# Linear attention's causal part: sub-chunks of 64 tokens in 32x64 and 64x32 TensorE tiles, two chunks at a time

## The chip, the core and the metric

The kernel runs on one core of a Trainium2 chip. The metric is the device time of one execution in microseconds (us). A core has five engines that run side by side, each through its own instruction queue in order: TensorE (PE: matrix products into PSUM, with its weight loads, PEld), VectorE (DVE), ScalarE (ACT), GpSimd (POOL) and SyncE (SP, which issues the DMAs here). PSUM, where TensorE writes, has 8 banks of 512 f32 columns on 128 partitions.

## What is computed

Four blocks, one after another, on 8 sequences of 1024 tokens with 256 features; each block adds to its input. The first is a decoder layer with linear attention (16 heads of 16) and a dense part of width 1024, the second a dense part of width 1024, the third softmax attention with one head of 256, the fourth a gated dense part of width 704 whose operands are rounded to a 4-bit format. The change is in the attention of the first block:

```python
q = sigmoid(heads(Wq, bq)); k = sigmoid(heads(Wk, bk)); v = heads(Wv, bv)
...                                            # scales from running sums of q and k
qs = q * (sink_in / normal)[..., None]
vs = v * src_comp[..., None]
kv = jnp.cumsum(jnp.einsum('bhld,bhlm->bhldm', k, vs), axis=2)
x  = jnp.einsum('bhld,bhldm->bhlm', qs, kv) * sink_alloc[..., None]
```

For token l this is the sum over all earlier tokens and itself of (qs_l . k_j) vs_j, head by head. A kernel splits it by chunks of tokens: inside a chunk the scores k.q are computed and cut to the causal triangle, and everything before the chunk enters through one carried state, the sum of k times vs (16 x 16 per head).

## The kernel before

All work is written as Python generators ("parts"), which ask for an engine, operands, PSUM banks and buffers; `Plan.run` picks, one after another, the part that can go on soonest by its own table of costs (`Plan.took`), so the order of the instructions on all engines is fixed when the program is built. Every instruction is issued through one helper, so that nearly all have one line in the profile (342); tile names tell them apart. Three things in the planner matter below. A need may carry `banks=n` and waits until so many banks are free. `took` counts a matmul with at most 32 rows or columns of weights as a quarter of a full one, and adds 0.2 where tiled and full matmuls follow each other; `run` lets tiled work follow tiled work. Where it expects TensorE to wait for more than 1.6 us, `fill` puts matmuls of the identity (bank<-ident in the profile) into the gap, one for each 0.22 of pause - 0.7.

Tokens go in chunks of 128 (`P`); four chunks make a group (`G`), so a sequence has two groups and the whole 16 (`flows`, p). `linear_group` and `linear_span` compute q, k and the scales of one group, with the running sums on DVE in buffers of kind "flow" (512 columns wide, nine of them). Then `linear_chunk` does the causal part for each of the four chunks, and beside it the dense parts (`dense`: w_in, w_out, hidden), the softmax attention and the last block (`soft_chunk`: wqk, qT, prob, vt, wgT, wuT, wdT) of earlier groups go on.

`linear_chunk` (line 1147) in order:
- v of the chunk (bank<-wv,n0T), plus bias, times its scale, into one of four `v_pads`, whose heads stand in 32 columns of which 16 are zero;
- qz, two copies of q with either the even or the odd heads set to zero (ACT, two of 256 columns);
- scores: for each of four row tiles (32 rows, two heads) and both halves k of the features a matmul of 32 rows by 128 columns with 256 columns moving, into four banks (bank<-qz,k, 8 matmuls);
- DVE multiplies each bank by the triangle `triu` into a flow buffer (sc<-bank,triu, four of 512 columns). In the first group ACT does it, with a large negative triangle (`later`, bf16) put into the bank first and a Relu;
- k is turned (two transposes and an ACT copy), except in a sequence's last chunk;
- into one bank: the carried state times q (bank<-q,kv_sum, 8 matmuls of 128 rows by 32 columns, 128 moving), then the chunk's own part (bank<-sc,v_pad, 16 of the same shape), and into its other columns the chunk's update of the state (bank<-v_pad,k, 8, 32 columns moving);
- ACT copies the result out (xo), DVE multiplies the update by the block diagonal (kv<-bank,bdiag), and POOL adds it to the carried sum in a new tile (kv_sum);
- the output projection (bank<-wo,xo), layer norm and the turn of the result for the dense part.

`count["attended"]` keeps the chunks in their order.

## Time and profile before

| | |
|---|---|
| median of 3 runs | 2615.89 us (2615.59 to 2617.68) |
| the profiled execution | 2618.8 us |
| its span, first to last instruction | 2617.1 us |
| granted TensorE clock, mean | 0.997 |
| evictions sc<-bank,triu on DVE | 240 of 680 ns |
| kv<-bank,bdiag on DVE | 56 of 420 ns |
| kv_sum adds on POOL | 48 of 728 ns (median) and 8 copies of 396 ns |
| bank<-ident on TensorE | 274 records, 35.1 us busy |

The profile is of one execution on the chip. It lists busy time by engine and by group of instructions: "out<-in" are the program's tile names, then the shape of the tile of weights (rows*columns), the output shape, the number of records, busy us and mean ns of one. Matmuls are pipelined, so a record's ns is its length from start to end, while the next one starts long before; busy us counts overlapping records once. PEld is the load of weights that goes with each matmul. Times in the timeline are us from the span's start.

### The profile page before, as it was taken

What the parts mean: (1) busy time and instruction counts of PE and PEld (TensorE: products, weight loads), DVE (VectorE), ACT (ScalarE), POOL (GpSimd) and SP (SyncE); (2) the same over time, 40 slices, a digit from 0 to 9 for tenths busy, and PEclk for the clock granted to TensorE, in tenths of its full rate; (3) what the DMA queues carried; (4) which work ended last, traced back from release to release, by engine and by line L of the source; (5) the groups of instructions that cost most, each with busy time, mean ns of one, the idle gap of its engine ahead of it and who ended that gap; (6) DMA issues with size and microseconds to landing.
All of it is one profiled execution on the core that took longest, in us unless ns stands there. A gap on an engine that the chain in (4) does not pass through costs nothing.

```text
span 2617.1 us, 46326 instructions
## 1 busy us (share of the span) xinstructions
PE 2571.5 (98%) x16593; PEld 2010.4 (77%) x16593; DVE 1947.3 (74%) x4352; ACT 1344.0 (51%) x2658; POOL 703.0 (27%) x1293
## 2 busy tenths in 40 slices
PE   8998999999999999999999999999999999999999
PEld 7777777877777777777877877777777777878777
DVE  6788796867769587685868768677785877855687
ACT  3535636464475544645555464645545545454443
POOL 2343332332313232131321322313231231311000
PEclk9999999999999999999999999999999999999999
DMA  2445443333323342322433323333333423333100
GB/s 75 125 121 154 115 117 95 109 88 107 86 80 101 85 115 68 108 80 85 117 81 92 97 75 99 92 108 81 99 82 83 115 72 96 88 87 89 31 5 21
DMA packets 391268, 237.11 MB, mean 91 GB/s; under 512 B 129152, under 2 KB 379520, under 8 KB 391040
## 3 DMA queue, kind: packets, MB, share of 16 engines
q1 hardware_dynamic: 391040, 234.16, 33.1%
q8 instruction: 132, 2.16, 0.4%
q14 instruction: 96, 0.79, 0.1%
HBM read 188.17 MB, written 20.71 MB: 80 GB/s over the span
## 4 chain that ended last, share of the span: by engine, by line
PE 80%; DVE 13%; ACT 3%; DMA 1%; issue 1%; POOL 1%; SPq 0%; DVEq 0%; POOLq 0%; ACTq 0%
PE bank L342 80%; DVE hid L342 2%; DVE prod L342 2%; DVE n L342 1%; ACT L342 1%; DVE ln_st L342 1%; DVE u L342 1%; DVE res L342 1%; DVE ln_mv L342 0%; DVE x_amax L342 0%; DMA spread<-packed 0%; DVE div L342 0%; DVE spread L342 0%; DVE mx L342 0%; DMA spun<-cut 0%
## 5 line engine op out<-in xcount | busy, mean ns | idle before, releaser
L342 PE MATMUL bank<-half,w_in 128*128 128x256 f32 x2048 | 533.4, 384 | 7.3 <-DVE v L342 4.5
L342 PE MATMUL bank<-w_out,hidden 128*128 128x256 f32 x2048 | 529.4, 383 | 2.7 <-DMA w_out<-in_L_ffn_w_dram 1.6
L342 POOL TENSOR_SCALAR ln_ve<-ln_mv 128x1 f32<-128x1 f32 x384 | 96.9, 252 | 1607.8 <-DVE ln_mv L342 1591.3
L342 PEld LDWEIGHTS bank<-w_out,hidden 128*128 128x128 f32 x2048 | 374.0, 190 | 105.2 <-issue 53.2
L342 PEld LDWEIGHTS bank<-half,w_in 128*128 128x128 f32 x2048 | 384.3, 191 | 85.6 <-issue 22.5
L342 ACT ACT_TABLE_LOAD x321 | 411.8, 1283 | 17.3 <-DVE nmax L342 11.6
L342 ACT ACTIVATE hidden<-bank,c_L_ffn_b 128x256 f32<-128x256 f32 x256 | 120.6, 472 | 269.4 <-PE bank L342 269.1
L342 POOL TENSOR_TENSOR ln_rstd<-ln_ve,neghalf 128x1 f32<-128x1 f32 x384 | 236.3, 615 | 32.0
L342 PE MATMUL bank<-n2T,qT 128*128 128x512 f32 x512 | 241.6, 594 | 0.4 <-ACT qT L342 0.2
L342 PE MATMUL bank<-vt,probT 128*128 128x256 f32 x1024 | 232.0, 380 | 0.0
L342 PEld LDWEIGHTS bank<-vt,probT 128*128 128x128 f32 x1024 | 193.1, 190 | 30.2 <-issue 3.0
L342 ACT ACTIVATE hidden<-bank,c_L_attn_b 128x256 f32<-128x256 f32 x256 | 119.7, 468 | 183.3 <-PE bank L342 182.8
L342 PE MATMUL bank<-wdT,hqT 128*128 128x256 f32 x768 | 176.6, 380 | 1.2 <-ACT hqT L342 1.0
L342 PE MATMUL bank<-wgT,xqT 128*128 128x352 f32 x512 | 173.8, 462 | 0.0
L342 PE MATMUL bank<-wuT,xqT 128*128 128x352 f32 x512 | 172.4, 459 | 0.0
L342 ACT COPY half<-spun 128x512 uint16<-128x512 uint16 x128 | 86.3, 674 | 150.1 <-DMA spun<-cut 149.6
L342 PEld LDWEIGHTS bank<-wdT,hqT 128*128 128x128 f32 x768 | 145.3, 190 | 22.7 <-ACT hqT L342 1.4
L342 DVE TENSOR_TENSOR sc<-bank,triu 128x512 f32<-128x512 f32 x240 | 149.7, 680 | 8.5 <-PE bank L342 8.0
L342 PEld LDWEIGHTS bank<-n2T,qT 128*128 128x128 f32 x512 | 93.4, 190 | 69.1 <-issue 60.5
L342 PEld LDWEIGHTS bank<-wuT,xqT 128*128 128x128 f32 x512 | 97.4, 190 | 54.1
L342 DVE TENSOR_TENSOR hid<-hid,bank 128x352 f32<-128x352 f32 x116 | 59.7, 515 | 101.4 <-PE bank L342 79.2
L342 PEld LDWEIGHTS bank<-wgT,xqT 128*128 128x128 f32 x512 | 93.7, 190 | 37.1 <-issue 4.3
(220 smaller groups left out, 4530.2 us busy)
## 6 DMA issues: line engine op xcount, KB each, us to landing
w_in<-in_L_attn_W_dram SPq DMA_DIRECT2D x256, 128.0 KB
w_out<-in_L_attn_W_dram SPq DMA_DIRECT2D x256, 128.0 KB
w_in<-in_L_ffn_w_dram SPq DMA_DIRECT2D x256, 128.0 KB
w_out<-in_L_ffn_w_dram SPq DMA_DIRECT2D x256, 128.0 KB
spread<-packed SPq DMA_DIRECT2D x90, 256.0 KB
x<-in_L_attn_inputs_dram SPq DMA_DIRECT2D x64, 128.0 KB
xr<-in_L_attn_inputs_dram SPq DMA_DIRECT2D x64, 128.0 KB
rows<-res SPq DMA_DIRECT2D x64, 128.0 KB
```

The lines of the kernel that those rows point to most:

```text
L342: ins = method(*args, **kw)
```

## The change

A chunk of 128 is cut into two sub-chunks of 64 (u = 0, 1), and two chunks (n = 0, 1) are done in one part, `linear_pair`. Scores are computed only inside a sub-chunk: 32 rows by 64 columns of weights, 128 columns moving (both heads' copies of 64 tokens), sub-chunk u on partitions 64u to 64u+63, the four row tiles in four banks; one bank now holds both chunks, so DVE masks four banks for a pair, with a triangle of 64 by 64. The update of the state is computed for each of the four sub-chunks, in tiles of 64 rows by 32 columns, before the scores; DVE brings it out in two operations (one per u, both chunks), and POOL turns the four updates into four running states, in place, one add after another. The chunk's own part takes 64 rows by 32 columns with 64 columns moving, and then each sub-chunk adds its state times q, 128 rows by 32 columns, 64 moving. The two u write two banks, and two ACT copies put them together in xo. What follows, `linear_rest`, is as before for each chunk. The turning of k moves ahead of the scores, and happens for all chunks.

Buffers: six of kind flow instead of nine, three of a new kind kvs, five weight buffers (`W_FF`) instead of four for each of w_in and w_out. The planner's table counts a tile's share of the array, with a least cost of 0.0136, and 0.2 at each change of tile shape.

```diff
-W_FF = 4
+W_FF = 5
...
-    "flow": (9, 512, F32),
+    "flow": (6, 512, F32),
+    "kvs": (3, 512, F32),
...
-            tiled = op == "matmul" and (kw["lhsT"].shape[-1] <= 32 or kw["lhsT"].shape[0] <= 32)
-            if tiled or op == "matmul" and kw["lhsT"].dtype == BF16:
-                cost *= 0.25
+                if rows * cols < P * P and kw["lhsT"].shape[-1] > 1:
+                    tiled = rows, cols
+                    cost = max(cost * rows * cols / (P * P), 0.0136)
...
+        yield pe(*pads, *kTs, *[t for t, _ in qzs], banks=2, tiled=True)
+        kvbanks = [mm_bank()[:, :D].rearrange("p (c k d) -> p c k d", c=2, k=2) for _ in range(2)]
+        for n in range(2):
+            for k in range(2):
+                for r in range(4):
+                    for u in range(2):
+                        sub = slice(64 * u, 64 * u + 64)
+                        nc.tensor.matmul(
+                            kvbanks[u][32 * r : 32 * r + 32, n, k, :32],
+                            lhsT=kTs[n][sub, k, 32 * r : 32 * r + 32],
+                            rhs=v_columns(pads[n][sub], range(4 * k + r, 4 * k + r + 1)),
...
+        yield pe(banks=4, tiled=True)
         banks = [mm_bank() for _ in range(4)]
...
-        for r, bank in enumerate(banks):
-            rows = slice(32 * r, 32 * r + 32)
+        for n in range(2):
             for k in range(2):
-                nc.tensor.matmul(
-                    bank[:, k * D : (k + 1) * D],
-                    lhsT=qk[1][rows, k, here],
-                    rhs=qz[rows, k, :, :],
+                for u in range(2):
+                    for r, bank in enumerate(banks):
+                        rows = slice(32 * r, 32 * r + 32)
+                        t0 = pair[n] * P + 64 * u
+                        nc.tensor.matmul(
+                            bank[64 * u : 64 * u + 64, n * D + k * P : n * D + (k + 1) * P],
+                            lhsT=qk[1][rows, k, t0 : t0 + 64],
+                            rhs=qzs[n][1][rows, k, :, 64 * u : 64 * u + 64],
...
+        for m in range(3 if end else 4):
+            before, after_ = states[m][1], states[m + 1][1]
+            if before is not None:
+                yield plan.pool(*[t for t, _ in states[m : m + 2]])
+                nc.gpsimd.tensor_tensor(after_, before, after_, ALU.add)
...
+        outs = [mm_bank()[:, :D].rearrange("p (c k t) -> p c k t", c=2, k=2) for _ in range(2)]
+        for n in range(2):
             for k in range(2):
+                for e in range(2):
+                    for r in range(4):
+                        for u in range(2):
+                            sub = slice(64 * u, 64 * u + 64)
+                            nc.tensor.matmul(
+                                outs[u][32 * r : 32 * r + 32, n, k, :],
+                                lhsT=pads[n][sub, 8 * k + 2 * r + e, :],
+                                rhs=scores[r][sub, n, k, e, :],
...
+        for n in range(2):
+            for u in range(2):
+                state = states[2 * n + u][1]
+                if state is None:
+                    continue
+                t0 = pair[n] * P + 64 * u
+                for k in range(2):
+                    for r in range(4):
+                        nc.tensor.matmul(
+                            outs[u][32 * r : 32 * r + 32, n, k, :],
+                            lhsT=state[:, k, 32 * r : 32 * r + 32],
+                            rhs=qk[0][:, k, t0 : t0 + 64],
```

More of the change, by code (lines that the diff above doesn't have):

```diff
@@ L181, in took @@
             cost = size * (0.853e-3 if op == "transpose" else 1.687e-3)
-            tiled = op == "matmul" and (kw["lhsT"].shape[-1] <= 32 or kw["lhsT"].shape[0] <= 32)
-            if tiled or op == "matmul" and kw["lhsT"].dtype == BF16:
-                cost *= 0.25
+            tiled = False
+            if op == "matmul":
+                rows, cols = (kw["lhsT"].shape[0], kw["lhsT"].shape[-1])
+                rows, cols = (min([n for n in (32, 64, P) if n >= x] + [P]) for x in (rows, cols))
+                if rows * cols < P * P and kw["lhsT"].shape[-1] > 1:
+                    tiled = rows, cols
+                    cost = max(cost * rows * cols / (P * P), 0.0136)
+                elif kw["lhsT"].dtype == BF16:
+                    cost *= 0.25
             if tiled != self.tiled:
@@ L465, in block_stack_kernel @@
     make_block_diagonal(tc.nc, bdiag, DH)
-    triu = const.tile([P, P], F32, name="triu")
-    make_upper_triangular(tc.nc, triu)
+    triu = const.tile([P, 64], F32, name="triu")
+    for u in range(2):
+        make_upper_triangular(tc.nc, triu[64 * u : 64 * u + 64])
     v_pads = [const.tile([P, H, 32], F32, name=f"v_pad{i}") for i in range(V_PADS)]
@@ L534, in late_constants @@
         nc.vector.tensor_scalar(
-            later[:, :GT].rearrange("p (n t) -> p n t", n=4),
-            triu.unsqueeze(1).to_broadcast([P, 4, P]),
+            later[:, :GT].rearrange("p (n t) -> p n t", n=8),
+            triu.unsqueeze(1).to_broadcast([P, 8, 64]),
             -1.0,
@@ L1143, in linear_span, with linear_pair @@
         plan.start(scaled(), p + 0.55 + after)
-        for i in span:
-            plan.start(linear_chunk(p, i, n0T, comp, qk), p + 0.55 + 0.03 * i + after)
-    def linear_chunk(p, i, n0T, comp, qk):
+        for j in range(span.start // 2, span.stop // 2):
+            plan.start(linear_pair(p, j, n0T, comp, qk), p + 0.55 + 0.06 * j + after)
+    def linear_pair(p, j, n0T, comp, qk):
         s, g = divmod(p, NG)
-        past, c = seqs[s]["past"], p * G + i
-        at = p - (p == 0 and i < 2)
-        here = slice(i * P, (i + 1) * P)
-        yield pe(
-            n0T,
-            banks=1,
-            when=lambda: count["v"] == c and c - count["attended"] < V_PADS and "v" in late,
-        )
-        bank = mm_bank()
-        for k in range(2):
-            nc.tensor.matmul(
-                bank[:, :D],
-                lhsT=n0T[:, k, here],
-                rhs=wqkv[2][:, k, :],
-                start=k == 0,
-                stop=k == 1,
-            )
-        count["v"] += 1
-        pad = v_pads[c % V_PADS]
-        v = yield from fresh("lin", dve(bank), "v")
-        nc.vector.tensor_tensor(v, bank[:, :D], bv1, ALU.add)
-        yield dve(comp)
-        nc.vector.tensor_tensor(
-            v_columns(pad, range(H // 2)),
-            v.rearrange("p (j e d) -> p j e d", e=2, d=DH),
-            comp[:, i, H:].rearrange("p (j e) -> p j e", e=2).unsqueeze(3)
-            .to_broadcast([P, H // 2, 2, DH]),
-            ALU.mult,
-        )
-        plan.drop(v)
-        tile_qz = yield from fresh(
-            "flow",
-            act(
-                qk[0],
-                at=at + 0.62 + 0.06 * i,
-                when=lambda: i in groups[p]["scaled"]
-                and count["scored"] == c
-                and c - count["attended"] < 2,
-            ),
-            "qz",
-        )
-        count["scored"] += 1
-        qz = tile_qz.rearrange("p (k e t) -> p k e t", k=2, e=2)
-        by_act = p == 0
-        for e in range(2):
-            nc.scalar.activation(
-                qz[:, :, e, :], qk[0][:, :, here], AF.Copy, scale=parity[:, e : e + 1]
-            )
-        yield pe(qz, *([later] if by_act else []), banks=4, tiled=not by_act)
@@ new lines, in linear_pair @@
+        past, c = seqs[s]["past"], p * G + 2 * j
+        at = p - (p == 0 and j == 0)
+        pair = (2 * j, 2 * j + 1)
+        pads, kTs = [], []
+        end = g == NG - 1 and j == G // 2 - 1
+        for n, i in enumerate(pair):
+            here = slice(i * P, (i + 1) * P)
+            yield pe(
+                n0T,
+                banks=1,
+                at=at + 0.55 + 0.06 * i,
+                when=lambda: count["v"] == c + n
+                and c + n - count["attended"] < V_PADS
+                and "v" in late,
+            )
+            bank = mm_bank()
+            for k in range(2):
+                nc.tensor.matmul(
+                    bank[:, :D],
+                    lhsT=n0T[:, k, here],
+                    rhs=wqkv[2][:, k, :],
+                    start=k == 0,
+                    stop=k == 1,
+                )
+            count["v"] += 1
+            pad = v_pads[(c + n) % V_PADS]
+            pads.append(pad)
+            v = yield from fresh("lin", dve(bank), "v")
+            nc.vector.tensor_tensor(v, bank[:, :D], bv1, ALU.add)
+            yield dve(comp)
+            nc.vector.tensor_tensor(
+                v_columns(pad, range(H // 2)),
+                v.rearrange("p (j e d) -> p j e d", e=2, d=DH),
+                comp[:, i, H:].rearrange("p (j e) -> p j e", e=2).unsqueeze(3)
+                .to_broadcast([P, H // 2, 2, DH]),
+                ALU.mult,
+            )
+            plan.drop(v)
@@ new lines, in linear_pair @@
+        for n, i in enumerate(pair):
+            yield pe(
+                banks=1,
+                at=at + 0.62 + 0.06 * i,
+                when=lambda: i in groups[p]["scaled"] and count["attended"] == c,
+            )
+            bank = turned([qk[1][:, k, i * P : (i + 1) * P] for k in range(2)])
+            kT = two((yield from fresh("lin", act(bank), "k")))
+            nc.scalar.copy(kT, bank)
+            kTs.append(kT)
+        qzs = []
+        by_act = p == 0
+        for n, i in enumerate(pair):
+            tile_qz = yield from fresh("flow", act(qk[0], at=at + 0.64 + 0.06 * i), "qz")
+            qz = tile_qz.rearrange("p (k e t) -> p k e t", k=2, e=2)
+            for e in range(2):
+                nc.scalar.activation(
+                    qz[:, :, e, :],
+                    qk[0][:, :, i * P : (i + 1) * P],
+                    AF.Copy,
+                    scale=parity[:, e : e + 1],
+                )
+            qzs.append((tile_qz, qz))
@@ new lines, in linear_pair @@
+        kv = past.get("kv")
+        sums = [None, None]
+        yield pe(*pads, *kTs, *[t for t, _ in qzs], banks=2, tiled=True)
[9 more added lines that the diff above has]
+                            rhs=v_columns(pads[n][sub], range(4 * k + r, 4 * k + r + 1)),
+                            start=n == 0 and k == 0,
+                            stop=True,
+                            skip_group_check=True,
+                        )
@@ L1201, in linear_chunk @@
+        plan.drop(*kTs)
+        yield pe(banks=4, tiled=True)
         banks = [mm_bank() for _ in range(4)]
@@ L1207, in linear_chunk @@
                 )
-        for r, bank in enumerate(banks):
-            rows = slice(32 * r, 32 * r + 32)
+        for n in range(2):
             for k in range(2):
-                nc.tensor.matmul(
-                    bank[:, k * D : (k + 1) * D],
-                    lhsT=qk[1][rows, k, here],
-                    rhs=qz[rows, k, :, :],
-                    start=not by_act,
-                    stop=True,
-                    skip_group_check=True,
-                )
-        plan.drop(tile_qz)
+                for u in range(2):
[6 more added lines that the diff above has]
+                            rhs=qzs[n][1][rows, k, :, 64 * u : 64 * u + 64],
+                            start=not by_act,
+                            stop=True,
+                            skip_group_check=True,
+                        )
+        plan.drop(*[t for t, _ in qzs])
+        for u in range(2):
+            new = yield from fresh("kvs", dve(kvbanks[u]), "kv")
+            new = sums[u] = new.rearrange("p (c k d) -> p c k d", c=2, k=2)
+            nc.vector.tensor_tensor(
+                new.rearrange("p c k (r d) -> p (c k) r d", r=4),
+                kvbanks[u][:, :, :, :32].rearrange("p c k d -> p (c k) d")
+                .unsqueeze(2).to_broadcast([P, 4, 4, 32]),
+                bdiag.rearrange("p (r d) -> p r d", r=4).unsqueeze(1).to_broadcast([P, 4, 4, 32]),
+                ALU.mult,
+            )
+        states = [(kv, kv if kv is None else kv[:, 1])]
+        for m in range(4):
+            tile_ = sums[m % 2]
+            states.append((tile_, tile_[:, m // 2]))
+        for m in range(3 if end else 4):
[3 more added lines that the diff above has]
+                nc.gpsimd.tensor_tensor(after_, before, after_, ALU.add)
+        past["kv"] = sums[1]
         scores = []
@@ L1222, in linear_chunk @@
             sc = yield from fresh("flow", (act if by_act else dve)(bank), "sc")
-            sc = sc.rearrange("p (n t) -> p n t", n=4)
+            scores.append(sc.rearrange("p (c k e t) -> p c k e t", c=2, k=2, e=2))
+            sc = sc.rearrange("p (n t) -> p n t", n=8)
             if by_act:
-                nc.scalar.activation(sc, bank.rearrange("p (n t) -> p n t", n=4), AF.Relu)
-                scores.append(sc)
+                nc.scalar.activation(sc, bank.rearrange("p (n t) -> p n t", n=8), AF.Relu)
                 continue
@@ L1229, in linear_chunk @@
                 sc,
-                bank.rearrange("p (n t) -> p n t", n=4),
-                triu.unsqueeze(1).to_broadcast([P, 4, P]),
+                bank.rearrange("p (n t) -> p n t", n=8),
+                triu.unsqueeze(1).to_broadcast([P, 8, 64]),
                 ALU.mult,
             )
-            scores.append(sc)
-        end = g == NG - 1 and i == G - 1
-        if not end:
-            yield pe(banks=1, at=at + 0.66 + 0.06 * i, when=lambda: count["attended"] == c)
-            bank = turned([qk[1][:, k, here] for k in range(2)])
-            kT = two((yield from fresh("lin", act(bank), "k")))
-            nc.scalar.copy(kT, bank)
-        kv = past.get("kv")
         yield pe(
-            pad,
+            *pads,
             *scores,
-            *([] if kv is None else [kv]),
-            *([] if end else [kT]),
-            banks=1,
+            *[t for t, _ in states[:4] if t is not None],
+            banks=2,
             tiled=True,
@@ L1250, in linear_chunk @@
         )
-        kv = past.get("kv")
-        both = mm_bank()
-        plan.keep(both)
-        bank = both[:, :D]
-        for k in range(2):
-            for r in range(4):
-                if kv is not None:
-                    nc.tensor.matmul(
-                        bank[32 * r : 32 * r + 32, k * P : (k + 1) * P],
-                        lhsT=kv[:, k, 32 * r : 32 * r + 32],
-                        rhs=qk[0][:, k, here],
-                        start=k == 0,
-                        stop=False,
-                        skip_group_check=True,
-                    )
@@ L1268, in linear_chunk @@
-        for k in range(2):
-            for e in range(2):
-                for r in range(4):
-                    nc.tensor.matmul(
-                        bank[32 * r : 32 * r + 32, k * P : (k + 1) * P],
-                        lhsT=pad[:, 8 * k + 2 * r + e, :],
-                        rhs=scores[r][:, 2 * k + e, :],
-                        start=kv is None and k == 0 and e == 0,
-                        stop=k == 1 and e == 1,
-                        skip_group_check=True,
-                    )
@@ L1279, in linear_chunk @@
-        plan.drop(*scores)
-        if not end:
-            kvbank = both[:, D : D + 64].rearrange("p (k d) -> p k d", k=2)
-            for k in range(2):
-                for r in range(4):
-                    nc.tensor.matmul(
-                        kvbank[32 * r : 32 * r + 32, k, :],
-                        lhsT=kT[:, k, 32 * r : 32 * r + 32],
-                        rhs=v_columns(pad, range(4 * k + r, 4 * k + r + 1)),
-                        start=False,
-                        stop=True,
-                        skip_group_check=True,
-                    )
-            plan.drop(kT)
@@ L1294, in linear_chunk @@
-        xo = two((yield from fresh("lin", act(bank), "xo")))
-        nc.scalar.copy(xo, two(bank))
-        if not end:
-            new = two((yield from fresh("lin", dve(kvbank), "kv")))
-            nc.vector.tensor_tensor(
-                new.rearrange("p k (r d) -> p k r d", r=4),
-                kvbank.unsqueeze(2).to_broadcast([P, 2, 4, 32]),
-                bdiag.rearrange("p (r d) -> p r d", r=4).unsqueeze(1).to_broadcast([P, 2, 4, 32]),
-                ALU.mult,
-            )
-            plan.let_go(both)
-            yield plan.pool(new)
-            total = past["kv"] = wk.tile([P, 2, P], F32, tag="kv_sum", name="kv_sum", bufs=2)
-            if kv is None:
-                nc.gpsimd.tensor_copy(total, new)
-            else:
-                nc.gpsimd.tensor_tensor(total, kv, new, ALU.add)
-            plan.drop(new)
-        else:
-            plan.let_go(both)
@@ L1314, in linear_chunk @@
-        count["attended"] += 1
-        if by_act and i == G - 1:
-            plan.drop(later)
-        yield pe(xo, banks=1, at=at + 0.7 + 0.06 * i, when=lambda: "chunk" in late)
+        outs = [mm_bank()[:, :D].rearrange("p (c k t) -> p c k t", c=2, k=2) for _ in range(2)]
+        for n in range(2):
+            for k in range(2):
+                for e in range(2):
+                    for r in range(4):
+                        for u in range(2):
+                            sub = slice(64 * u, 64 * u + 64)
[3 more added lines that the diff above has]
+                                rhs=scores[r][sub, n, k, e, :],
+                                start=n == 0 and k == 0 and e == 0,
+                                stop=False,
+                                skip_group_check=True,
+                            )
@@ new lines, in linear_pair @@
+        for n in range(2):
+            for u in range(2):
+                state = states[2 * n + u][1]
+                if state is None:
+                    continue
+                t0 = pair[n] * P + 64 * u
+                for k in range(2):
+                    for r in range(4):
+                        nc.tensor.matmul(
+                            outs[u][32 * r : 32 * r + 32, n, k, :],
+                            lhsT=state[:, k, 32 * r : 32 * r + 32],
+                            rhs=qk[0][:, k, t0 : t0 + 64],
+                            start=False,
+                            stop=True,
+                            skip_group_check=True,
+                        )
@@ new lines, in linear_pair @@
+        plan.drop(*scores, sums[0])
+        if kv is not None:
+            plan.drop(kv)
+        if end:
+            plan.drop(sums[1])
+        xo = yield from fresh("flow", act(*outs), "xo")
+        xo = xo.rearrange("p (c k t) -> p c k t", c=2, k=2)
+        for u in range(2):
+            nc.scalar.copy(xo[:, :, :, 64 * u : 64 * u + 64], outs[u])
+        count["attended"] += 2
+        if by_act and j == G // 2 - 1:
+            plan.drop(later)
+        left = [2]
+        for n, i in enumerate(pair):
+            plan.start(linear_rest(p, i, xo, xo[:, n], left), at + 0.7 + 0.06 * i)
@@ L1318, in linear_chunk, with linear_rest @@
+    def linear_rest(p, i, tile_xo, xo, left):
+        at = p - (p == 0 and i < 2)
+        yield pe(tile_xo, banks=1, when=lambda: "chunk" in late)
         bank = mm_bank()
@@ L1322, in linear_chunk @@
             )
-        plan.drop(xo)
+        left[0] -= 1
+        if not left[0]:
+            plan.drop(tile_xo)
         count["linear"] += 1
```

## The prediction

> **What bounds the kernel now.** I read the page's shares of busy time first, then the groups of TensorE instructions by form, then the timeline of one chunk, then narrow windows inside its bursts.

> ```profile
> span 2617.1 us, 46326 instructions
> PE 2571.5 (98%) x16593; PEld 2010.4 (77%) x16593; DVE 1947.3 (74%) x4352; ACT 1344.0 (51%) x2658; POOL 703.0 (27%) x1293
> PE 80%; DVE 13%; ACT 3%; DMA 1%; issue 1%; POOL 1%; SPq 0%; DVEq 0%; POOLq 0%; ACTq 0%
> ```

> TensorE is busy for 98% of the span and carries 80% of the chain that ended last; the other engines have room (74%, 51%, 27%). So time that TensorE no longer needs comes off the end nearly one for one, as long as the instruction order keeps feeding it. The groups that the change touches:

> ```profile
> L342 PE MATMUL bank<-qz,k 32*128 32x256 f32 x1024 | 75.6, 400 | 1.3 <-ACT qz L342 1.3
> L342 PE MATMUL bank<-sc,v_pad 128*32 128x128 f32 x2048 | 67.8, 273 | 0.0
> L342 PE MATMUL bank<-q,kv_sum 128*32 128x128 f32 x896 | 36.1, 279 | 0.0
> L342 PE MATMUL bank<-v_pad,k 128*32 128x32 f32 x896 | 17.3, 195 | 0.0
> ```

> Together 197 us busy, 7.5% of the span. An f32 matmul of the program is two records (64 chunks x 8 score matmuls are x1024). The timeline shows what one chunk costs, start to start:

> ```profile
> 1004.88 1.06 PE L342 MATMUL bank<-n2T,wqk 128*128 128x128 f32 x8
> 1005.86 0.65 PE L342 MATMUL bank<-q,kv_sum 128*32 128x128 f32 x16
> 1006.33 1.06 PE L342 MATMUL bank<-sc,v_pad 128*32 128x128 f32 x32
> 1007.20 0.31 PE L342 MATMUL bank<-v_pad,k 128*32 128x32 f32 x16
> 1007.44 1.17 PE L342 MATMUL bank<-qz,k 32*128 32x256 f32 x16
> 1008.53 1.13 PE L342 MATMUL bank<-half,w_in 128*128 128x256 f32 x4
> 1009.50 1.03 PE L342 MATMUL bank<-wo,xo 128*128 128x256 f32 x4
> 1010.36 1.03 PE L342 MATMUL bank<-w_out,hidden 128*128 128x256 f32 x4
> ```

> Four full records of 256 columns take 0.86 us (1009.50 to 1010.36): 0.845 ns per column. Four tiles at once give for sc,v_pad 32 x 128 x 0.845 / 4 = 0.865 us against 0.87 seen, so column tiles run truly side by side. For q,kv_sum it is 0.43 against 0.47, for qz,k 0.865 against 1.09, for v_pad,k 0.11 against 0.24. What is over is the change of tile mode: qz,k stands between two modes and pays 0.22 us.

> Last, the step from record to record inside one turn of the tiles (each line: a window, its length, then TensorE matmuls and weight loads, busy us and, as x, how many touch the window; the two columns that follow are of no use here), for row tiles and then for column tiles:

> ```profile
> 1007.43:1007.45 0.02, 0.01 (x1) 0.01 (x2) 0.00 (x0) 1.00 0.00 0
> 1007.43:1007.46 0.03, 0.02 (x2) 0.03 (x2) 0.00 (x0) 1.00 0.00 0
> 1007.43:1007.47 0.04, 0.03 (x3) 0.04 (x3) 0.00 (x0) 1.00 0.00 0
> 1007.43:1007.48 0.05, 0.04 (x4) 0.04 (x4) 0.00 (x0) 1.00 0.00 0
> ...
> 1007.19:1007.25 0.06, 0.06 (x16) 0.06 (x12) 0.00 (x0) 1.00 0.00 0
> 1007.19:1007.30 0.11, 0.11 (x22) 0.11 (x16) 0.00 (x0) 1.00 0.00 0
> ```

> The four row tiles of qz,k start about 13 ns apart (the fourth within 0.05 us of the window's start). Column tiles of v_pad,k add 6 records in 0.05 us; the group's 0.31 us less one record's 195 ns, over 15 steps, is 7.7 ns, and within a turn it is about 7 ns. With eight tiles these steps may become the limit; before, they never were.

> [...]

> **The change part by part.** Sums are made against the profiled execution (2618.8 us, span 2617.1, so 1.7 around it), which stands 2.9 above the median 2615.9; I carry the difference over to the median.

> 1. Array time before: 64 chunks x (0.865 scores + 0.865 sc) + 56 x (0.43 + 0.11), eight chunks having no carried state and eight no update = 110.7 + 30.2 = 140.9 us.
> 2. After, per pair of chunks. Scores: 64 records x 128 columns x 0.845 / 8 tiles = 0.865. sc: 128 records, array 6.8 ns each, step 6.9 taken = 0.88. Update: 64 records of 32 columns, array 3.4 ns, so the step binds: 64 x 6.9 = 0.44. Over 32 pairs: 70 us. State matmuls: 960 of the program, 1920 records x 64 x 0.845 / 4 = 26 us. Sum 96. Gain 44.9 us. The halving of scores and of sc (masked blocks above the diagonal are no longer computed) pays; the state part doubles its use (one per 64 tokens at half the columns: same time) and the update grows.
> 3. Mode changes: walking the instruction order of the two built programs, neighbouring TensorE groups change tile shape 301 times before and 293 after: 8 x 0.2 = 1.6 us gained. [...]
> 4. Sequence 0's first group: 8 instead of 16 bf16 mask matmuls, 4.1 us / 16 each: 2 us gained. All 64 chunks are turned, not 56: 16 transposes at 109 ns (the row of 2 takes 0.22 us, 1003.14 to 1003.36): 1.7 lost.
> 5. DVE: 120 of 240 masked evictions of 680 ns go, 82 us of instruction time; the 56 kv evictions of 420 ns become 64 of 512 elements, nearest row 680 ns: 20 added. Net about 62 us off a 74% engine beside the path: I count 0, bounds 5 gained and 2 lost. ACT: 8 copies more (0.37 each), 8 evictions and 6 table warm-ups less: nothing.
> 6. POOL: 48 adds of 728 ns and 8 copies become 112 in-place adds: 43 us more on an engine at 27%. They are serial, four a pair, 2.9 us, and behind them in POOL's queue stand the layernorms' ln_ve and ln_rstd, for which DVE waits, and the turns of h. The state matmuls need all; they were moved behind the sc matmuls' own inputs, four DVE evictions (2.7 us), which cover the adds. Uncovered it is 0.2 us a pair, 6 us; I take 0.
> 7. Buffers and queues: flow 9 to 6, a pair taking 2 qz and 4 sc; a fifth weight buffer on SP's loads can win back the 1.9 us that TensorE waits for w_out at most; I take 0. A pair holds 2 + 4 of the 8 PSUM banks at a time.
> 8. Stalls: the built programs hold filler matmuls (bank<-ident) where the order expects TensorE to idle. There are 137 before, 182 after. The first four stretches are alike; then 69 in 5 stretches become 114 in 9. A filler is 35.1 us / 137 = 0.26 us (the busy time of bank<-ident in the groups by form), and each stretch leaves some 0.7 us unfilled (the code's pause - 0.7): 45 x 0.22 to 0.26 + 4 x 0.7 = 13 us lost. All lie in the first eighth of the order, where there is little other work and a pair must finish before the next: the latency of two chunks is now exposed at once. Bounds 5 and 25.

> Sum: -44.9 - 1.6 - 2 + 1.7 + 13 = -33.8, span 2583.3, execution 2585.0, at the median **2582 us**.

> **Rivals.**
> - Little of it is kept (banks and latency): the queue is full of other work after 400 us (199.85 of 200 us busy from 400 to 600), against. For: six banks held at once, with up to two accumulators of the dense layers and two score banks of softmax kept besides. If every pair stalls TensorE 0.8 us more, 32 x 0.8 = 26: 2608.
> - Row tiles step at 13.4 ns (16 x 0.84, as qz,k's 13) in the new 64x32 bursts too, where each record changes the row group: sc 128 x 13.4 = 1.72, update 0.86, 1.25 us a pair more, 40 us: 2622, the gain gone. Scores still fit (8 x 13 = 104 of 108 ns).
> - The other side, slower: the step grows with the rows passed. qz,k's 13 ns is per 32 rows, so two 64-row tiles would be 27 ns apart, alternating with a 7 ns step back: 17 ns a record over the (64 + 128) x 32 = 6144 records of update and sc: 6144 x 10.1 ns = 62: 2644. It decides from a mean step of 6.9 + 33.8 us / 6144 = 12.4 ns. Against both: the scores of before stagger once per turn and lose nothing to it over the turn's 216 ns, so 13 ns may be a start offset and not a rate.

> **How the numbers follow.** Forecast 2582: 0.60, own range 2565 to 2602. Little kept: 0.12. Step 13.4 ns: 0.14. Growing step: 0.14. The range 2562 to 2624 takes the first three nearly whole. About 5 us (0.2%) is what a measurement of this kernel can tell from no change: faster 0.69 (the forecast and three quarters of the second), same 0.10 (rest of the second, half of the third), slower 0.21.

> **What would show it.** Right: scores bursts of 64 records at about 1.1 us start to start [...], sc of 128 at 0.9 to 1.0, update of 64 at 0.5 to 0.6, and these groups' busy sum near 130 us instead of 197; fillers and idle longer before 300 us, none after. Wrong: sc bursts of 1.7 us or more (step), bursts as computed but TensorE idle on evictions after 400 us (banks), or POOL kv as releaser of the state matmuls.

## The result and the profile after

The changed kernel takes 2642.33 us in the median of 4 runs (2641.62 to 2642.94) against 2616.56 for the kernel before: ratio 1.0098, 95% interval 1.0081 to 1.0116. It is slower by 1%, where 1.3% faster was forecast, and outside the forecast's range. From the page of its profiled execution, with the queue that it lists as instruction (q8):

```profile
span 2639.9 us, 56960 instructions
PE 2558.4 (97%) x21937; PEld 2005.1 (76%) x21939; DVE 1913.1 (72%) x4240; ACT 1310.1 (50%) x2632; POOL 748.2 (28%) x1351
...
q8 instruction: 174, 2.85, 0.4%
...
PE 78%; DVE 10%; DMA 3%; ACT 3%; issue 2%; POOL 0%; SPq 0%; DVEq 0%; ACTq 0%
```

TensorE is busy 13 us less than before, but the span is 23 us longer: its idle time went from 46 to 82 us. There are 5344 more matmul records, and q8 brought 174 blocks instead of 132, each of 16384 bytes in both traces. The groups of the change, from the TensorE groups by form:

```profile
L349 PE MATMUL bank<-sc,v_pad 64*32 64x64 f32 x4096 | 49.6, 225 | 2.7 <-ACT sc L349 1.6 <-DVE sc L349 1.2
...
L349 PE MATMUL bank<-qz,k 32*64 32x128 f32 x2048 | 39.4, 283 | 0.0
...
L349 PE MATMUL bank<-q,kv 128*32 128x64 f32 x1920 | 36.9, 221 | 21.5 <-issue 21.5
...
L349 PE MATMUL bank<-v_pad,k 64*32 64x32 f32 x2048 | 24.3, 201 | 0.0
```

Their busy sum is 150 us, not the 130 of the forecast, and ahead of q,kv stands 21.5 us of idle time that no engine and no DMA of the kernel released ("issue"). Where this lies is seen in the timeline of one pair:

```profile
1355.18 1.48 PE L349 MATMUL bank<-sc,v_pad 64*32 64x64 f32 x128
...
1356.60 0.98 PE L349 MATMUL bank<-q,kv 128*32 128x64 f32 x53
1359.38 0.41 PE L349 MATMUL bank<-q,kv 128*32 128x64 f32 x11 [1.81 <-issue]
```

The sc burst takes 1.42 us to the next start; 0.88 to 1.0 was expected. Then TensorE stops inside a burst, after 53 of its 64 matmuls, for 1.8 us; the matmul that goes on waits for no semaphore in the trace. Windows from just before that sc burst, and from just before the update burst of another pair, show their pace (the length of the window; then busy us and, as x, how many TensorE matmuls, then weight loads, had begun by its end):

```profile
1355.15:1355.43 0.28, 0.25 (x32) 0.25 (x33) 0.00 (x0) 0.00 (x0) 1.00 0.00 0
1355.15:1355.63 0.48, 0.45 (x44) 0.45 (x48) 0.00 (x0) 0.00 (x0) 1.00 0.00 0
1355.15:1356.23 1.08, 1.05 (x106) 1.05 (x109) 0.00 (x0) 0.00 (x0) 1.00 0.36 121
...
886.32:886.50 0.18, 0.17 (x32) 0.18 (x33) 0.00 (x0) 1.00 0.69 216
886.32:886.56 0.24, 0.23 (x32) 0.24 (x33) 0.00 (x0) 1.00 0.70 226
886.32:886.80 0.48, 0.47 (x55) 0.47 (x57) 0.00 (x0) 1.00 0.86 290
```

32 records of sc start in the first 0.25 us, nearly as reckoned, then only 12 in the next 0.2 us, and from there 62 in 0.6 us, about 10 ns a record. In the update too, 32 records start in the first 0.18 us. Then neither a matmul nor a weight load begins for at least 0.06 us, and afterwards 23 records start in 0.24 us. So the pace breaks once, after 32 records, and is lower behind the break.

Third, other waits of TensorE (us in total, times, longest). In the kernel before they were none, 0.7 and 4.5 us in total:

```profile
PE bank L349 <- issue: 22.5, 14, 2.4
PE bank L349 <- DVE n L349: 10.4, 7, 1.9
PE bank L349 <- DVE v L349: 7.9, 5, 2.2
```

Adding up the steps from each TensorE record's start to the next gives an account of both spans, but for some 6.6 us at their two ends (a step far over its group's usual length is cut there and the excess put under idle; fillers are not cut):

| us | before | after | difference | forecast |
|---|---|---|---|---|
| the four groups, changes of tile shape included | 167.6 | 143.2 | -24.4 | -46.5 |
| fillers bank<-ident | 38.0 | 50.6 | +12.6 | +13 with what they leave open |
| idle beyond the usual step | 36.6 | 71.1 | +34.5 | in the line above |
| all other matmuls | 2368.2 | 2368.4 | +0.2 | 0 |

So about 22 us of the gain did not come, and 34 us of idle time did. Of the idle time after, 20.4 us lie inside q,kv, where there was none before, and 18.3 before ident,n and half,w_in, where DVE's n and v are late (5.2 before). The first row still holds stalls shorter than its cut: bursts that nothing disturbs take 165.1 us in sum before and 134.7 after.

### The profile page after: what moved, and what is told of

Read it like the earlier page. It is cut to its first block, busy times and chain, and to the rows that moved or that the text cites. A ratio compares the mean times of both kernels' runs of the same rounds, so it can differ in the third digit from the quotient of the medians.

```text
span 2639.9 us, 56960 instructions
## 1 busy us (share of the span) xinstructions
PE 2558.4 (97%) x21937; PEld 2005.1 (76%) x21939; DVE 1913.1 (72%) x4240; ACT 1310.1 (50%) x2632; POOL 748.2 (28%) x1351
## 4 chain that ended last, share of the span: by engine, by line
PE 78%; DVE 10%; DMA 3%; ACT 3%; issue 2%; POOL 0%; SPq 0%; DVEq 0%; ACTq 0%
PE bank L349 78%; DVE prod L349 2%; ACT L349 2%; DVE hid L349 1%; DMA spread<-packed 1%; DMA spun<-cut 1%; DMA packed<-scale 1%; DVE n L349 1%; DVE ln_st L349 1%; DVE x_amax L349 0%; DVE spread L349 0%; DVE u L349 0%; DVE div L349 0%; DVE w_raw L349 0%; SPq L349 0%
## 5 line engine op out<-in xcount | busy, mean ns | idle before, releaser
L349 POOL TENSOR_TENSOR ln_rstd<-ln_ve,neghalf 128x1 f32<-128x1 f32 x384 | 229.8, 599 | 31.9
L349 DVE TENSOR_REDUCE mx<-bank 128x1 f32<-128x512 f32 x128 | 86.5, 676 | 40.3 <-PE bank L349 40.2
```

The source lines that it names most:

```text
L349: ins = method(*args, **kw)
```

## The experiments

Three theories. **Supply**: after the first records of a burst TensorE gets its instructions no faster than one per 4 to 5 ns (an estimate from the 8 to 10 ns a record behind the break; a record is two, a weight load and a matmul), and in long runs of short matmuls the next block of instructions comes late. **Row groups**: the third rival of the prediction, whose 2644 us lies next to the result. **Order**: new waits come from an order planned with too small costs.

### Row groups

In the update and in sc the loop over u goes outside r, so that the row group changes after four matmuls and not after each (shown for sc).

```diff
                 for e in range(2):
-                    for r in range(4):
-                        for u in range(2):
+                    for u in range(2):
+                        for r in range(4):
```

> The update and sc bursts change the row group after every fourth record instead of after every record (loop u moved outside r); same instructions, same order of bursts. Row groups (a change of row group costs the step): update burst of 64 records from 0.69 us to about 0.5, sc burst of 128 from 1.41 to about 1.0, 32 x 0.6 = 19 us faster than the changed kernel. Supply (TensorE gets instructions too slowly once the ones queued ahead are used up): both bursts unchanged within 0.05 us, time unchanged at 2642, the 2 us gaps inside q,kv still there (about 20 us in sum).

Measured: 2639.16 us, ratio to before 1.0096 (1.0081 to 1.0111). Its groups:

```profile
L349 PE MATMUL bank<-sc,v_pad 64*32 64x64 f32 x4096 | 49.9, 225 | 2.9 <-ACT sc L349 1.6 <-DVE sc L349 1.2 <-issue 0.2
...
L349 PE MATMUL bank<-v_pad,k 64*32 64x32 f32 x2048 | 24.2, 199 | 0.0
```

49.9 against 49.6 us and 24.2 against 24.3; start to start 1.41 and 0.69 us as before the edit. So the rival whose number came out nearest has the wrong mechanism: its 2644 us was luck.

### The same pace without row tiles

The kernel before, its update issued four times as often, into columns that nothing reads.

```diff
+            for c in range(1, 4):
+                again = both[:, D + 64 * c : D + 64 * c + 64].rearrange("p (k d) -> p k d", k=2)
+                for k in range(2):
+                    for r in range(4):
+                        nc.tensor.matmul(
+                            again[32 * r : 32 * r + 32, k, :],
...
```

> The kernel before, with the update's eight matmuls (128x32 tiles, 32 columns) issued three times more into unused columns of its bank, so the burst v_pad,k has 64 records instead of 16, without any row tile. Supply: the first 30 or so records step at 7 ns and the later ones at 8 to 17, burst 0.65 us or more. Row groups: all at 7 to 7.7 ns, burst about 0.24 + 48 x 7.2 ns = 0.58 us and no step after the first 32.

```profile
1007.39 0.74 PE L342 MATMUL bank<-v_pad,k 128*32 128x32 f32 x64
1008.06 1.17 PE L342 MATMUL bank<-qz,k 32*128 32x256 f32 x16
```

64 records take 0.67 us to the next start, and the one run 2646.31 us. Inside, the first 25 start as in the kernel before (7 ns apart, 12 between turns of four), the rest in pairs 17 ns apart, 8.4 ns a record, with column tiles only. The length is the supply theory's, but alone it settles little: with its 12 ns between turns the fast part already takes 7.8 ns a record, so turns of 33 ns for four tiles all the way would give nearly the same. The changed kernel's update decides against that: its first 32 records come at 5.3 ns on average, their weight loads no slower, and behind the break they too come in pairs 17 ns apart. So neither the tiles nor the loads need the longer step.

### Long runs

The same with fourteen more updates instead of three: 240 records in a row.

> The kernel before, with its update's eight matmuls issued fourteen times more into unused columns of the bank: 240 records of 128x32 tiles in a row after 48 others, with no row tile, no pair and no POOL add inside. Supply with late blocks of instructions: steps of 7 ns for some 30 records, 8.4 after, and in many of the 56 bursts one gap of 1 to 2.5 us between 120 and 230 records after the run's start. If the gaps of the changed kernel belong to its own states or banks: no gap here, bursts of 2.1 us.

```profile
1137.12 1.06 PE L342 MATMUL bank<-v_pad,k 128*32 128x32 f32 x102
1139.33 1.42 PE L342 MATMUL bank<-v_pad,k 128*32 128x32 f32 x128 [1.15 <-issue]
1142.80 0.37 PE L342 MATMUL bank<-v_pad,k 128*32 128x32 f32 x10 [2.05 <-issue]
```

```profile
L342 PE MATMUL bank<-v_pad,k 128*32 128x32 f32 x13440 | 144.0, 200 | 121.9 <-issue 121.9
```

The gaps appear here without pairs, without row tiles in the burst and without adds of POOL, and sum to 122 us; the one run took 2907.23 us. The burst shown pauses after 102 records and again after 128 more, and in all seven bursts with two gaps exactly 128 records lie between: 128 records are 256 instructions, a matmul and a weight load each. q8 brought 230 blocks here against 132 in the kernel before; 1.61 MB for 56 x 14 x 8 x 4 = 25088 more instructions is 64 bytes each, so a block (2.16 MB / 132 = 16 KB) is 256 of them. TensorE's own matmuls and weight loads, 33186 before, 43876 in the changed kernel and 58250 here, would fill 130, 171 and 228 blocks; q8 brought 132, 174 and 230. In the changed kernel each of the 12 long gaps inside q,kv began 0.3 to 0.9 us after the start of a transfer on q8, which took 0.9 to 1.8 us, and TensorE went on 1.3 to 1.6 us after that transfer's end; here, after all 63 gaps, it went on 1.2 to 1.6 us after one. Such transfers are 14 us apart in the median of the changed kernel. So the gap is a wait for instructions. Two gaps in one burst were not expected.

### Other work before the state matmuls

Six full matmuls of other work must have been issued between sc and the states (not in the first two groups, nor at a sequence's end); `plan.full` counts them.

```diff
+        mark = plan.full
+        yield pe(when=lambda: p < 2 or end or plan.full >= mark + 6)
         for n in range(2):
             for u in range(2):
                 state = states[2 * n + u][1]
```

> Between the sc burst (128 records) and the state matmuls (64) at least six full matmuls of other work are issued (not in the first two groups, nor at the end of a sequence). Supply, with late blocks of instructions: the gaps inside q,kv fall from 20 us to under 5, two more changes of tile mode cost 22 x 0.2 = 4 us, sum 10 to 15 us faster than the changed kernel (about 2630). Late states (the gap is a wait for POOL's adds): the gaps go as well, but POOL's adds must then end within 1 us of the gap in the changed kernel. Neither: gaps stay, 4 us slower.

Measured: 2616.43 us, ratio 1.0004 (0.9995 to 1.0012), the whole loss against before regained.

```profile
L351 PE MATMUL bank<-q,kv 128*32 128x64 f32 x1920 | 35.3, 221 | 8.4 <-issue 6.5 <-POOL cut L351 1.7
```

The gaps in q,kv fell from 20.4 to 7.8 us in the account, not quite under the 5 expected for supply. What is left lies where the edit does not reach: of the 11 state bursts that still follow sc at once, five stand still for 1.5 to 2.0 us; of the 21 with other work between, none for more than 0.35 us. Late states are not the cause: in the changed kernel POOL's last add had ended at least 1.2 us before each of the 32 state bursts began. TensorE's idle time from 300 to 2200 us is the window's length less the first busy time, for the kernels before, changed, and with the gap:

```profile
300.00:2200.00 1900.00, 1884.14 (x12171) 1468.71 (x12170) 1417.66 (x3125) 1009.99 (x1957) 530.08 (x961) 1.00 0.34 93
```

```profile
300.00:2200.00 1900.00, 1854.34 (x16062) 1446.02 (x16051) 1372.86 (x2995) 975.42 (x1916) 563.97 (x1002) 1.00 0.34 92
```

```profile
300.00:2200.00 1900.00, 1882.81 (x16390) 1467.49 (x16389) 1395.69 (x3046) 1004.45 (x1955) 580.25 (x1025) 1.00 0.35 95
```

16, 46 and 17 us. The gain is 26 us, more than the 13 of the gaps and more than the 10 to 15 expected: in the new order the waits for DVE's n fell from 10.4 to 1.4 and those for v are gone from the longer waits as well, while the fillers rose from 50.6 to 62.6. So half of the gain is shown to be supply; the other half came with another order.

### The order's costs

```diff
-                    cost = max(cost * rows * cols / (P * P), 0.0136)
+                    cost = max(cost * rows * cols / (P * P), 0.0215 if rows < P else 0.0136)
```

> The planner's least cost of a matmul in row tiles raised from 0.0136 to 0.0215 us, what the bursts measured; the same work in another order. If the 14 us of other new waits (for n, v, prob) come from an order made with wrong times: those waits fall by 5 to 15 us and the time to about 2630. If they come from real lateness of DVE or DMA: unchanged within 5 us.

Measured: ratio 1.0048 (1.0029 to 1.0067), 13 us faster than the changed kernel (five runs from 2621.00 to 2633.91; the profile is of the slowest). The wait for n fell to 0.7 us, the one for v is gone from the longer waits, and the gaps in q,kv stayed (22.7 us). So those two waits belong to the order. Both edits together:

> The gap before the state matmuls and the raised cost of row tiles together. If the two act on different losses: gaps in q,kv under 9 us as with the gap alone, waits for n and v under 8, time 2605 to 2612. If the gain of the gap run came from a luckier order and not from the instruction supply: above 2620.

Measured: 2626.41 us, ratio 1.0037 (1.0024 to 1.0049), worse than the gap alone. That is what the second theory said, and it speaks for a luckier order as a good part of the gap run's gain. The supply itself is not refuted: the gaps are down as with the gap alone (7.5 us of idle time inside q,kv, all in bursts that follow sc at once), and other waits rose (10.9 us before half,w_in, 8.1 before ident,w_raw). The two edits do not add up: each orders the rest anew, and that is worth 10 us either way.

### Buffers

The changed kernel with W_FF back at 4:

> The changed kernel with four weight buffers instead of five. If the fifth buffer brings something: 2 to 6 us slower than the changed kernel. If more loads on SP's queue ahead of the spread transfers make DVE late: 5 to 10 us faster. Both small: within 4 us, with the q,kv gaps and the burst lengths unchanged in either case.

Measured: ratio 1.0144 (1.0124 to 1.0163), 12 us slower than with five, twice what was expected. Of its waits, one of 2.8 us is for a load of w_in, and those for w_raw rose from 6.2 to 11.8. The kernel before with five (and eight flow buffers):

> The kernel before with five weight buffers (and eight flow buffers instead of nine, to make room), nothing else changed. If the 12 us that the changed kernel loses without its fifth buffer are a gain of that buffer in itself: 5 to 12 us faster than before. If they belong to the changed kernel's order alone: within 4 us of before.

Measured: ratio 1.0018 (1.0009 to 1.0028), 5 us slower, just outside the second theory's 4; here one flow buffer went as well. The fifth buffer is no gain by itself; in the changed kernel's order it is.

### The first groups

The old part, masked on ACT, in the first four groups; then the pairs. With the gap:

```diff
+EARLY = 4
...
-        for j in range(span.start // 2, span.stop // 2):
+        if p < EARLY:
+            for i in span:
+                plan.start(linear_chunk(p, i, n0T, comp, qk), p + 0.55 + 0.03 * i + after)
+        else:
+          for j in range(span.start // 2, span.stop // 2):
             plan.start(linear_pair(p, j, n0T, comp, qk), p + 0.55 + 0.06 * j + after)
```

> The gap kernel, with the first four of the sixteen groups (two sequences) done by the old single-chunk part, all masked on ACT. If the fillers and waits of the first 300 us come from pairs exposing the latency of two chunks: fillers and early stalls fall by 15 to 25 us, a quarter of the burst gain (6 us) is given up, time 2598 to 2606, faster than both kernels. If they come from something else: 2616 to 2622.

Measured: 2612.88 us, ratio 0.9985 (0.9978 to 0.9993): faster than both kernels, by less than expected. Fillers are 42.8 us against 62.6 with the gap alone, the idle sum fell by 3, the four matmul groups of the change cost 4.6 more. What the expectation left out are the matmuls that put the mask into the banks where ACT masks:

```profile
L352 PE MATMUL bank<-later 128*128 128x512 bf16 x64 | 16.5, 380 | 0.0
```

With the gap alone there were 8 of them, 2.1 us; these 14 us take most of the gain away again. The same without the gap:

> The changed kernel with the old single-chunk part in the first four groups, without the gap before the state matmuls. If the two losses are separate: fillers 43 us as in the run with both, gaps in q,kv about three quarters of 20, so 15 us, and the time some 13 us above that run, near 2626. If the early part also carried the gain: near 2613.

Measured: 2639.04 us, ratio 1.0091 (1.0076 to 1.0106), not 13 but 26 us above the run with both. The gap is again worth 26 us; the early part alone only 2, although the fillers fell to 43.2: the mask matmuls cost it 15.6 us too, and 14.1 us of idle time inside q,kv and 14.1 of waits for n and v remain. With the gap and the old part in two groups only:

> The gap kernel with the old part in the first two groups only. Half of the given-up burst gain comes back (3 us), fillers as many as in the run with four groups (166): 2608 to 2614. If pairs in groups 2 and 3 still expose their latency: 2614 to 2622.

Measured: 2617.84 us, ratio 1.0011 (1.0004 to 1.0018), in the second theory's range, though its fillers are the 166 that the first one named. The mask matmuls are halved (7.8 us), but TensorE idles 9 us longer than with four groups; the largest rise is in the waits for the masked scores, from 2.4 to 6.5 us. With four groups, the gap and the raised cost:

> The run with the old part in four groups and the gap, with the planner's cost of row tiles raised to what the bursts measured. If the order made with right costs is better in general: 2600 to 2610. If, as the gap and the cost together showed, the order varies by some 10 us for other reasons: 2610 to 2625.

Measured: 2640.55 us, ratio 1.0098 (1.0081 to 1.0115), worse than either expectation. Waits for DVE's sc and hid are 14.8 and 8.4 us in this order, against 2.4 and 1.0 without the raised cost. Right costs of these bursts do not make the order good.

## Why the prediction was wrong

- **Where TensorE's time goes, and that it counts nearly one for one**: right. The 23 us of the longer span are all in TensorE's account.
- **Step 1 and the scores of step 2**: right. A scores burst of 64 takes 1.14 us to the next start (1.1 forecast), and the state burst without a gap 1.03, 0.17 over the 0.865 of its columns. A change of tile shape shows in full groups too: in the kernel before, four records of w_out,hidden take 0.864 us to the next start between full groups (median), 0.957 ahead of a tiled group and 0.967 behind one.
- **The step of 6.9 ns in step 2**: wrong, this is the term that was mis-sized. It is the step inside a turn of four tiles in v_pad,k of before; the prediction's own lines also have 7.7 ns as the mean of that burst of 16 records, which ends before the pace breaks. Over whole bursts the step measured 10.0 ns in sc and 9.0 in the update: (128 x 3.1 + 64 x 2.1) x 32 = 17 us. That is the whole shortfall of the undisturbed bursts: they gain 165.1 - 134.7 = 30.4 us where 46.5 were forecast. The other 6 of the 22 us are short stalls that the account leaves in that row. The pace breaks after 32 records in sc and update of the changed kernel, and in the two runs with a longer update after 25; what sets the place is not shown. Behind it a record takes 8.4 ns at best.
- **Steps 3 and 4**: as forecast as far as the traces show it: the mask matmuls take about 2 us where they took 4.1, and turning k has 146 records where it had 130. No run tested these steps by themselves.
- **Steps 5 and 6**: DVE's masks and updates changed as forecast, though its busy time fell by only 34 us; POOL rose by 45. No wait of the states for POOL appears; the cover held.
- **Step 7**: the fifth buffer was set at 0 to 1.9 us; taking it away cost 12. The estimate looked at the waits of the order before, and the order was another.
- **Step 8**: the fillers were right (+12.6). That stalls lie only in the first eighth was wrong: the idle time from 300 to 2200 us went from 16 to 46 us. 18 us of it is the supply in runs of 192 records, for which the prediction has no term, though the doubled number of records stood in it. The waits for n and v go away in an order whose costs have 0.0215 where the prediction's planner had 0.0136; why they came up in this one is not shown beyond that.
- **The rivals**: the growing step gave 2644 and names the bursts that did lose, but its cause is refuted, and its 17 ns would have made an sc burst 2.2 us long, not 1.41. The step of 13.4 ns is refuted by the same bursts. Banks held at once did not cost more in sum: TensorE's waits for DVE's v, kv and sc in front of matmuls that do not read them, which can only be for the bank, were 10.9 us before and are 10.6 after. In the last run above, though, the 14.8 us stand before n2T,wqk, which does not read sc either.

In sum: forecast -33.8 us of span, measured +22.8. The difference of 56.6 is 22 in the four matmul groups (17 of them the step), 20 of late instructions and 14 of other idle time. What limits TensorE to 8.4 ns a record the runs do not tell.

## What to carry to other kernels

Smaller tiles that leave out masked blocks lower the array's time and multiply the instructions: here the scores went from 75.6 to 39.4 us busy and from 1024 to 2048 records. Compare the new time of a whole burst with its number of instructions, not with the step of a short burst, and break long runs of short matmuls with long ones: in the run with the gap the 21 state bursts with other work before them had no stop over 0.35 us, while five of the other 11 stood for 1.5 to 2.0. In a kernel with an order planned ahead, a changed cost or buffer moves all waits; here that alone was worth 10 us and more in either direction, so test the mechanism by its own bursts and gaps and not by the total.
